# ScalarE reads s2 in VectorE's PSUM bank instead of in a copy of its own

## The chip, the cores and the metric

The kernel runs on one core of a Trainium2 chip. Its engines are TensorE (PE, matrix products), VectorE (DVE), ScalarE (ACT), GpSimd (POOL) and SyncE (SP, which issues DMAs). PE writes its products into PSUM, which has eight banks of 512 float32 values per partition; DVE and ACT read and write PSUM and SBUF, and in this kernel POOL works on SBUF alone. The metric is the device time of one execution in microseconds (us).

## The reference

Four graph layers follow each other on an input x of 64 graphs, 256 nodes and 128 features, each with a layer norm, a ReLU and a residual. The first layer holds nearly all the work:

```python
W1, W2 = (W[:, :F], W[:, F:])
s1 = jnp.einsum('bkf,ef->bke', x, W1)
s2 = jnp.einsum('bkf,ef->bke', x, W2)
pre = s1[:, :, None, :] + s2[:, None, :, :] + b_lin
h = jnp.where(pre >= 0, pre, ALPHA * pre)
e = jnp.einsum('bije,e->bij', h, a) + bias
attn = jax.nn.softmax(e, axis=2)
out = jax.nn.sigmoid(jnp.einsum('bij,bjf->bif', attn, x))
```

For every pair of nodes (i, j) of a graph, and for each of 256 features e, s1 of node i and s2 of node j are added and put through a leaky ReLU; a weighted sum over e gives one number per pair. That is 64 x 256 x 256 x 256 elements. The other layers (a second attention layer, an attention with tanh and exp, and a gated recurrent layer of five steps) are small beside it.

## The kernel before

**Pairs.** The features lie on the partitions, in two halves (`ec` 0 and 1). For one node i and one half, the value for all 256 nodes j is one instruction over a 128x256 tile: s2 against a per-partition scalar of node i. Three engines make such tiles, into buffers named r (twelve of them; each holds eight tiles), with forms that differ by terms which are put right elsewhere:

- ACT: `activation(Relu, bias=s1)`, one tile per instruction (L698);
- POOL: `tensor_scalar` with min and max against s1n, the negated s1 (L703), from the SBUF tile s2;
- DVE: `tensor_tensor` max of s2 and s1n, four tiles (128x1024, a half) or eight (128x2048, a whole) per instruction (L680).

PE multiplies each r by a window of the weights and accumulates over all of them in the bank e_ps (L764). In some batches DVE first merges the second half's value into a tile that some engine has made, by a `scalar_tensor_tensor` (L722), so that PE has fewer products to do.

**Where s2 lies.** For each graph, `senders` (or `first_head` for the first) has PE write s2 into a PSUM tile s2_ps of 128x2x256 float32, which fills a bank. Two such banks take turns in a pool that other tiles share. ACT copies it to the SBUF tile s2 (L577, L497). Inside `Pairs`, `own` says which copy an engine reads: DVE reads s2_ps. ACT, at its second piece of work on a graph, copies s2 once more, into a tile s2_act in a PSUM bank of its own (L642); its first two pieces read the SBUF tile, and all later ones s2_act. POOL reads the SBUF tile.

**The order of the work.** The program is written in an order that a planner sets while the kernel is built. A `Model` keeps one clock per engine and adds a cost in nanoseconds for each instruction: 365 for an ACT tile from PSUM, 42 more from SBUF, 454 for a POOL tile, 1131 and 2198 for DVE's half and whole, 392 for a merge. The main loop always issues the piece that can start first by these clocks; a free engine takes the next half batch of the graph. The other layers run as chains of small steps (`Chain`), which are put among the pairs at a set pace. The instructions of each engine run on the chip in the order issued. The semaphores between engines are set by the layer below the kernel, from which instruction writes and reads which tile or bank in that order; the kernel's text has none.

Of the kernel before, what the change touches and what calls it, by code (L numbers as in the profile page):

```python
# [8 lines left out]
F32 = mybir.dt.float32  # L9
# [3 lines left out]
P = 128  # L13
N = 256
# [41 lines left out]
def kernel(ctx: ExitStack, tc: tile.TileContext, ins: dict, out: bass.AP):  # L56
# [14 lines left out]
    ps_c = ctx.enter_context(tc.tile_pool(name="ps_c", bufs=1, space=bass.MemoryType.PSUM))  # L71
# [13 lines left out]
    model = Model()  # L85
# [7 lines left out]
    def act(n, pointers=0, sbuf=0, table=0, more=0):  # L93
        model.op("act", 50 + n * 0.832 + 69 * sbuf + (0, 75, 154)[pointers] + 11 * table + more)
        return nc.scalar
# [37 lines left out]
    def constant(shape, name):  # L133
        return const.tile(shape, F32, name=name)
# [20 lines left out]
    table = constant([P, 1], "table")  # L155
# [424 lines left out]
    class Pairs:  # L580
# [5 lines left out]
        def __init__(self, g, b, of, snd):  # L586
            self.g, self.b, self.of, self.snd = g, b, of, snd
            self.row = 0
            self.todo = []
            self.merges = []  # L590
            self.batches = []
            self.opened = False
            self.owned, self.by_act = {}, 0

            self.s1n_v = of["s1n"][:, :, bass.ts(b, N)].rearrange(
                "p c (k g t) -> p c g k t", k=2, g=4
            )
            self.s1n_b = of["s1n"][:, :, bass.ts(b, N)].rearrange(
                "p c (k g t) -> p c k g t", k=2, g=4
            )  # L600
# [31 lines left out]

        def own(self, who):

            if who == "dve":
                return self.snd["s2_ps"]
            if who == "act":

                self.by_act += 1
                if self.by_act == 2:  # L640
                    t = self.owned[who] = ps_c.tile([P, 2, N], F32, tag="s2_act", name="s2_act")
                    act(2 * N, table=1).copy(t, self.snd["s2"])  # L642
                if self.by_act <= 2:
                    return self.snd["s2"]
            return self.owned[who]

        def whole(self, batch, who):
            batch["halves"] += 1
# [10 lines left out]
        def make(self, who):  # L659

            if not self.todo:
                self.begin()
            batch, ec, g2 = self.todo.pop(0)
            if g2 == 0:
                batch["r"] = rp.tile([P, 4, 2, N], F32, tag="r", name="r")
                self.batches.append(batch)
            r, t = batch["r"], batch["t"]
            s2 = self.snd["s2"] if who == "pool" else self.own(who)
            s1, s1n = self.of["s1"], self.of["s1n"]
            if who == "dve":  # L670
                whole = g2 == 0 and self.todo and self.todo[0][0] is batch
                if whole:
                    self.todo.pop(0)
                n = 4 if whole else 2
                if batch["two"]:
                    s1n = self.s1n_b[:, ec, 1, 2 * g2 : 2 * g2 + n, t : t + 2].unsqueeze(3)
                else:
                    s1n = self.s1n_v[:, ec, 2 * g2 : 2 * g2 + n, :, t : t + 1]
                model.op("dve", model.WHOLE if whole else model.HALF)
                nc.vector.tensor_tensor(  # L680
                    r[:, 2 * g2 : 2 * g2 + n, :, :],
                    s2[:, ec : ec + 1, :].unsqueeze(1).to_broadcast([P, n, 2, N]),
                    s1n.to_broadcast([P, n, 2, N]),
                    ALU.max,
                )
                if whole:
                    if batch["merged"]:
                        self.merges.append((model.t[who] + LAG[who], batch, 0))
                        g2 = 1
                    else:  # L690
                        self.whole(batch, who)
            else:
                for g, ic, i in self.nodes(batch, g2):
                    if g > 2 * g2 or ic:
                        yield
                    if who == "act":
                        model.op("act", model.TILE["act"] + 42 * (s2 is self.snd["s2"]))
                        nc.scalar.activation(  # L698
                            r[:, g, ic, :], s2[:, ec, :], AF.Relu, bias=s1[:, ec, i : i + 1]
                        )  # L700
                    else:
                        model.op("pool", model.TILE["pool"])
                        nc.gpsimd.tensor_scalar(  # L703
                            r[:, g, ic, :], s2[:, ec, :], FLT_MAX, s1n[:, ec, i : i + 1],
                            ALU.min, ALU.max,
                        )
            if batch["merged"]:
                self.merges.append((model.t[who] + LAG[who], batch, g2))
            else:
                self.whole(batch, who)  # L710
# [601 lines left out]
```

## Time and profile before

| | |
|---|---|
| median of 3 runs | 5020.07 us (5019.8 to 5020.6) |
| profiled execution | 5019.59 us, span 5017.8 us |
| granted TensorE clock, mean | 0.999 |
| instructions | 176,085 |
| DMA | 29.56 MB, mean 6 GB/s |
| copies into s2_act (L642) | 64, 70.2 us busy, 1097 ns mean of a row |
| ACT reads of the SBUF tile s2 (L698) | 512, 298.2 us busy, 1006 ns mean of a row |

How to read it: a group of instructions has its line, engine, operation, tiles (output <- inputs), shapes and count; then busy time, the mean length of one row in ns, and the idle time just before them with what ended it. Rows of one engine overlap: an instruction is on record from its start to its last write, and the next starts before that, so the step from one to the next is shorter than the mean row. A line of the timeline merges equal instructions that follow each other: start, length from the first start to the last end, and their number; an idle time before it is in brackets, with what ended it.

### The profile page before, as it was taken

Reading aid. Unit: us, or ns where it says so; the run is one execution under the profiler, and the core shown is the slowest. Engines: PE = TensorE matmul, PEld = TensorE weight load, DVE = VectorE, ACT = ScalarE, POOL = GpSimd, SP = SyncE. Lnnn points to the kernel's source line nnn. Section 1 sums busy time; section 2 is a strip of 40 time slices with the busy share of each in tenths; the row PEclk is TensorE's granted clock in tenths of the full one; section 3 lists DMA queues with packets and bytes.
Section 4 is the critical chain, followed back from the end, with each engine's and each line's share of the span. In section 5 each row is a group of like instructions: output and inputs, shape, how many; then the busy total and the mean of one; then the engine's idle time right before and its main releaser. Section 6 shows DMA issues by size and latency. Waiting matters only on the chain.

```text
span 5017.8 us, 176085 instructions
## 1 busy us (share of the span) xinstructions
PE 4985.7 (99%) x69627; PEld 2291.3 (46%) x69627; DVE 4895.7 (98%) x8591; ACT 4922.9 (98%) x12912; POOL 4778.0 (95%) x10637
## 2 busy tenths in 40 slices
PE   9999999999999999999999999999999999999998
PEld 4444444444444444444444444444444444444444
DVE  9999999999999999999999999999999999999994
ACT  8999999999999999999999999999999999999994
POOL 8999999999999999999999999999999999999881
PEclk9999999999999999999999999999999999999999
DMA  0000000000000000000000000000000000000000
GB/s 22 4 6 2 5 6 7 6 2 6 7 6 7 2 6 6 7 6 2 6 8 4 7 4 6 6 7 4 4 6 6 7 7 2 5 5 4 4 4 8
DMA packets 56109, 29.56 MB, mean 6 GB/s; under 512 B 20336, under 2 KB 55280, under 8 KB 55280
## 3 DMA queue, kind: packets, MB, share of 16 engines
q1 hardware_dynamic: 54736, 18.04, 1.5%
q8 instruction: 546, 8.95, 0.7%
q14 instruction: 283, 2.32, 0.2%
q10 hardware_dynamic: 544, 0.26, 0.0%
HBM read 9.84 MB, written 8.45 MB: 4 GB/s over the span
## 4 chain that ended last, share of the span: by engine, by line
PE 92%; DVE 4%; ACT 3%; issue 1%; POOL 0%; DMA 0%; DVEq 0%; ACTq 0%; POOLq 0%
PE e_ps L764 56%; PE gate_ps L109 8%; PE hv_ps L109 6%; PE m_ps L109 5%; PE s_ps L109 3%; DVE r L680 3%; PE o_ps L109 2%; PE e_ps L109 2%; ACT r L698 2%; PE rc_ps L109 2%; PE hn_ps L116 1%; PE rsum_ps L109 1%; PE e_ps L116 1%; PE h_t_ps L116 1%; DVE r L722 1%
## 5 line engine op out<-in xcount | busy, mean ns | idle before, releaser
L703 POOL TENSOR_SCALAR r<-s,s1n 128x256 f32<-128x256 f32 x10012 | 4528.5, 476 | 79.4 <-PE e_ps L764 36.4
L698 ACT ACTIVATE r<-s_act,s 128x256 f32<-128x256 f32 x9664 | 4170.7, 871 | 7.6 <-PE e_ps L764 6.0
L764 PE MATMUL e_ps<-r,a_win 128*32 128x256 f32 (+1 forms) x40144 | 3258.1, 467 | 3.4 <-DVE r L680 3.3
L680 DVE TENSOR_TENSOR r<-s_ps,s1n 128x1024 f32<-128x1024 f32 (+1 forms) x1281 | 2291.0, 1824 | 3.9 <-PE e_ps L764 3.9
L764 PEld LDWEIGHTS e_ps<-r,a_win 128*32 128x32 f32 x40144 | 1279.9, 110 | 1574.3 <-issue 853.6
L722 DVE SCALAR_TENSOR_TENSOR r<-s_ps,s1n,r 128x256 f32<-128x256 f32 x4504 | 1852.6, 471 | 1.7 <-POOL r L703 1.0
L698 ACT ACTIVATE r<-s,s 128x256 f32<-128x256 f32 x512 | 298.2, 1006 | 0.1
L109 PE MATMUL m_ps<-adj_t,hn 128*32 128x256 f32 x4096 | 248.0, 381 | 1.6 <-ACT hn L1089 1.6
L455 ACT ACTIVATE h<-x,bsh,brs 128x128 f32<-128x128 f32 x384 | 229.6, 850 | 5.6 <-POOL bsh L449 4.7
L109 PEld LDWEIGHTS m_ps<-adj_t,hn 128*32 128x32 f32 x4096 | 133.0, 110 | 118.2 <-issue 32.2
L1066 ACT ACTIVATE gate_ps<-gate_ps,bz 128x512 f32<-128x512 f32 (+1 forms) x170 | 170.8, 1005 | 2.7 <-PE gate_ps L109 2.7
L1068 ACT ACTIVATE hv_ps<-hv_ps,bh 128x512 f32<-128x512 f32 (+1 forms) x170 | 166.4, 979 | 6.5 <-PE hv_ps L109 6.5
L1038 ACT COPY m_t<-m_ps 128x512 f32<-128x512 f32 (+1 forms) x170 | 161.4, 949 | 9.3 <-PE m_ps L109 9.3
L1048 ACT ACTIVATE m_ps<-gate_ps,br 128x512 f32<-128x512 f32 (+1 forms) x170 | 161.0, 949 | 8.9 <-PE gate_ps L109 7.2
L109 PE MATMUL hv_ps<-rh,u_th 128*32 128x512 f32 (+1 forms) x1360 | 168.4, 567 | 0.9 <-DVE rh L1051 0.9
L109 PE MATMUL gate_ps<-m_t,t_w_w 128*32 128x512 f32 (+1 forms) x1360 | 168.1, 568 | 0.3 <-ACT m_t L1038 0.2
L109 PE MATMUL hv_ps<-m_t,t_w_w 128*32 128x512 f32 (+1 forms) x1360 | 168.5, 567 | 0.0
L109 PE MATMUL gate_ps<-m_t,w_t 128*32 128x512 f32 (+1 forms) x1360 | 168.4, 568 | 0.0
L1089 ACT COPY hn<-hn_ps 128x512 f32<-128x512 f32 (+1 forms) x136 | 126.5, 930 | 18.2 <-PE hn_ps L116 18.0
L109 PE MATMUL gate_ps<-hf,u_t 128*32 128x512 f32 (+1 forms) x1088 | 135.4, 567 | 0.0
L109 PE MATMUL s_ps<-h0t,w_p 128*32 128x256 f32 (+1 forms) x1568 | 134.9, 445 | 0.5 <-ACT h0t L471 0.5
L447 POOL TENSOR_TENSOR brs<-bve,neg_half 128x4 f32<-128x4 f32 (+1 forms) x136 | 133.5, 982 | 0.0
(213 smaller groups left out, 4388.1 us busy)
## 6 DMA issues: line engine op xcount, KB each, us to landing
xt<-in_x_dram SPq DMA_DIRECT2D x30, 256.0 KB
out_dram<-y SPq DMA_DIRECT2D x30, 256.0 KB
row<-rows SPq DMA_DIRECT2D x128, 0.5 KB
xt<-in_x_dram SPq DMA_DIRECT2D x4, 128.0 KB
out_dram<-y SPq DMA_DIRECT2D x4, 128.0 KB
bound<-row SPq DMA_DIRECT2D x30, 2.0 KB
raw_L_gnn_w_w<-in_L_gnn_w_w_dram SPq DMA_DIRECT2D x3, 128.0 KB
adj_n<-in_adj_dram ACTq DMA_DIRECT2D x1, 256.0 KB
```

What stands on the lines that cost most here:

```text
L109: nc.tensor.matmul(out[bass.ts(c, 32), :], lhsT=lhsT[:, bass.ts(c, 32)], rhs=rhs, **flags)
L116: nc.tensor.transpose(out, src, ident)
L455: act(P, 2, 1).activation(h[:, g, :], xt[:, g, :], AF.Relu, bias=shift[:, g : g + 1], scale=rstd[:, g : g + 1],)
L680: nc.vector.tensor_tensor(r[:, 2 * g2 : 2 * g2 + n, :, :], s2[:, ec : ec + 1, :].unsqueeze(1).to_broadcast([P, n, 2, N]), s1n.to_broadcast ...
L698: nc.scalar.activation(r[:, g, ic, :], s2[:, ec, :], AF.Relu, bias=s1[:, ec, i : i + 1])
L703: nc.gpsimd.tensor_scalar(r[:, g, ic, :], s2[:, ec, :], FLT_MAX, s1n[:, ec, i : i + 1], ALU.min, ALU.max,)
L722: nc.vector.scalar_tensor_tensor(r[:, g, ic, :], self.own("dve")[:, 1, :], self.of["s1n"][:, 1, i : i + 1], r[:, g, ic, :], ALU.max, ALU.add,)
L764: nc.tensor.matmul(to, lhsT=a_win[:, sign, 31 - t : 63 - t], rhs=of, start=False, stop=self.over, skip_group_check=True,)
L1038: act(W).copy(m_t, m_ps)
L1048: act(W, 1).activation(t_r, g_ps, AF.Tanh, bias=br, scale=0.5)
L1066: act(W, 1).activation(t_z, g_ps, AF.Tanh, bias=bz, scale=0.5)
L1068: act(W, 1).activation(cand, hv_ps, AF.Tanh, bias=bh)
```

## The change

`own` gives DVE and ACT the same tile, s2_ps; the copy s2_act and the count of ACT's pieces are dropped. The planner's cost of an ACT tile loses the 42 ns for SBUF. POOL goes on reading the SBUF tile.

```diff
-            self.owned, self.by_act = {}, 0
...
         def own(self, who):
 
-            if who == "dve":
-                return self.snd["s2_ps"]
-            if who == "act":
-
-                self.by_act += 1
-                if self.by_act == 2:
-                    t = self.owned[who] = ps_c.tile([P, 2, N], F32, tag="s2_act", name="s2_act")
-                    act(2 * N, table=1).copy(t, self.snd["s2"])
-                if self.by_act <= 2:
-                    return self.snd["s2"]
-            return self.owned[who]
+            return self.snd["s2_ps"]
...
-                        model.op("act", model.TILE["act"] + 42 * (s2 is self.snd["s2"]))
+                        model.op("act", model.TILE["act"])
                         nc.scalar.activation(
                             r[:, g, ic, :], s2[:, ec, :], AF.Relu, bias=s1[:, ec, i : i + 1]
                         )
```

In the changed kernel the line numbers from L642 on are 11 lower: L698 becomes L687, L680 L669, L703 L692, L722 L711, L764 L753.

## The prediction

> **What bounds the kernel now.** I read the page's busy line first, then the groups kept apart by shape, the waits of ScalarE (ACT) and VectorE (DVE), and the timeline of the same microseconds on both engines.
>
> ```profile
> PE 4985.7 (99%) x69627; PEld 2291.3 (46%) x69627; DVE 4895.7 (98%) x8591; ACT 4922.9 (98%) x12912; POOL 4778.0 (95%) x10637
> ```
>
> All four engines are full at once; the planner has dealt the work out evenly, so no single stage sets the end. By shape, the work that touches s2 is this:
>
> ```profile
> L698 ACT ACTIVATE r<-s_act,s 128x256 f32<-128x256 f32 x9664 | 4170.7, 871 | 7.6 <-PE e_ps L764 6.0 <-POOL bmm L445 1.2
> L722 DVE SCALAR_TENSOR_TENSOR r<-s_ps,s1n,r 128x256 f32<-128x256 f32 x4504 | 1852.6, 471 | 1.7 <-POOL r L703 1.0 <-ACT r L698 0.5
> L680 DVE TENSOR_TENSOR r<-s_ps,s1n 128x2048 f32<-128x2048 f32 x738 | 1664.6, 2276 | 3.7 <-PE e_ps L764 3.7
> L680 DVE TENSOR_TENSOR r<-s_ps,s1n 128x1024 f32<-128x1024 f32 x543 | 644.2, 1210 | 0.3 <-PE e_ps L764 0.3
> ```
>
> ACT reads the bank s2_act, DVE the bank s2_ps. The last column says that ACT waited before its reads for 7.6 us in the whole run and DVE for 5.7, and no wait of ACT's reads on DVE is among them. The timeline of both engines shows why the span is short: they read side by side.
>
> ```profile
> 1009.64 4.98 ACT L698 ACTIVATE r<-s_act,s 128x256 f32<-128x256 f32 x12
> 1009.36 1.26 DVE L722 SCALAR_TENSOR_TENSOR r<-s_ps,s1n,r 128x256 f32<-128x256 f32 x3
> 1010.53 2.28 DVE L680 TENSOR_TENSOR r<-s_ps,s1n 128x2048 f32<-128x2048 f32 x1
> 1012.73 3.21 DVE L722 SCALAR_TENSOR_TENSOR r<-s_ps,s1n,r 128x256 f32<-128x256 f32 x8
> ```
>
> Twelve ACT reads run beside twelve DVE reads. Four more places give prices: the step of a read in a packed row, and what a start after a wait costs.
>
> ```profile
> 23.68 11.46 ACT L698 ACTIVATE r<-s_act,s 128x256 f32<-128x256 f32 x31
> 62.68 0.47 ACT L698 ACTIVATE r<-s_act,s 128x256 f32<-128x256 f32 x1
> ...
> 1002.95 4.37 DVE L722 SCALAR_TENSOR_TENSOR r<-s_ps,s1n,r 128x256 f32<-128x256 f32 x11
> 1007.24 1.21 DVE L680 TENSOR_TENSOR r<-s_ps,s1n 128x1024 f32<-128x1024 f32 x1
> 1008.37 0.47 DVE L722 SCALAR_TENSOR_TENSOR r<-s_ps,s1n,r 128x256 f32<-128x256 f32 x1
> ```
> ```profile
> 4980.82 0.45 ACT L1048 ACTIVATE m_ps<-gate_ps,br 128x256 f32<-128x256 f32 x1 [1.27 <-issue]
> 4981.30 0.42 DVE L1051 SCALAR_TENSOR_TENSOR rh<-m_ps,hf 128x256 f32<-128x256 f32 x1 [0.29 <-ACT m_ps L1048]
> ...
> 4935.81 0.48 DVE L834 TENSOR_SCALAR elu_m<-xh_ps,c_L_gnn_bi 128x256 f32<-128x256 f32 x1 [0.46 <-PE xh_ps L109]
> 4936.39 0.45 ACT L836 ACTIVATE xh_ps<-xh_ps,c_L_gnn_bi 128x256 f32<-128x256 f32 x1 [0.99 <-DVE elu_m L834]
> ```
>
> An ACT read alone takes 0.47 us, and one in a row steps by (11.46 - 0.47)/30 = 0.366. A DVE merge (L722) takes 0.47 alone and steps by (4.37 - 0.47)/10 = 0.39. The half read steps by 1008.37 - 1007.24 = 1.13 and the whole read by 1012.73 - 1010.53 = 2.20, each with a row 0.08 longer. A handover from ACT to DVE takes 4981.30 - 4981.27 = 0.03; the one from DVE to ACT here, where the wait is an instruction of its own, 4936.39 - 4936.29 = 0.10.
>
> **What the change does, part by part.** It removes 64 copies into s2_act (0.49 us a step, 31 us of ACT). It also ends the 512 ACT reads that went to SBUF before and beside the copy: they cost 298.2 us in their rows and step by about 0.40, so about 17 us go. The planner hears of 42 ns less on these and shifts a little work: in the instruction listing of the changed kernel ACT has 10,272 reads (before 10,176), POOL 9,980 (10,012), DVE 714 whole, 553 half and 4,592 merging reads (738, 543, 4,504). Taken alone, this is a gain of below 50 us on ACT.
>
> What it adds is not in the diff but in that listing, which names the semaphores that each instruction waits for. Two shortened excerpts from the middle (L687 is the old L698, L669 the old L680):
>
> ```
> ACT  L687 Activation r<-s_ps,s 128x256 [waits DVE]
> ACT  L687 Activation r<-s_ps,s 128x256 x4
> ACT  L687 Activation r<-s_ps,s 128x256 [waits DVE]
> DVE  L669 TensorTensor r<-s_ps,s1n 128x1024 [waits Activation]
> DVE  L669 TensorTensor r<-s_ps,s1n 128x2048 [waits Activation]
> ```
>
> Wherever, in program order, the reader of an s2_ps bank changes from one engine to the other, the second waits for the other's last read: 4,786 such waits on ACT and 4,795 on DVE. By its value, each names exactly the latest read of the other engine. Program order is the planner's order of time, in which both engines read alternately, and the planner knows nothing of the waits. So the two engines take turns over the bank, 9,581 times, and their read times add up instead of lying side by side. Behind a waiting read its engine's whole queue stands: for ACT the copies and activations of the other layers, for DVE the normalisations and gates; PE then waits for the batches, and POOL for the buffers that PE frees.
>
> The sum, made on the chain of turns:
> - Reads at packed steps: ACT 10,272 x 0.366 = 3,760; DVE 714 x 2.20 + 553 x 1.13 + 4,592 x 0.39 = 1,571 + 625 + 1,791 = 3,987. Together 7,747 us.
> - First read of a turn, not overlapped with its predecessor: ACT 4,786 x (0.47 - 0.366) = 498; DVE 4,795 x 0.08 = 384. Together 882.
> - Handovers: 7,486 waits sit on the reading instruction, at 0.03: 225. 2,095 sit on a wait instruction of their own, at 0.10: 210. Together 435.
> - Other work inside a turn, between two reads of the same turn, stretches it: 630 instructions of ACT, 267 us at their packed steps, and 70 of DVE, 17 us: 284.
> - Other work between two turns lies beside the other engine's turn: 1,804 instructions of ACT (817 us) and 2,603 of DVE (856 us). Turn by turn, only 29 us of it are longer than the turn that covers them. If nothing of it were covered it would cost 1,673.
> - Ends without turns, as now: 15.6 us ahead of the first read and 5,017.8 - 4,907.5 = 110 after the last: 126.
> - At changes of graph two banks are in use and 205 reads (some 78 us) have no partner to wait for; I take back 50.
> - Waits of the two engines for PE and POOL: between 100 and 4,870 us the waits views add up to some 50 us now. Other engines get slack (PE 4,986 and POOL 4,778 us of work in a span almost twice as long), so I keep 50, between 0 and twice that.
>
> Sum: 7,747 + 882 + 435 + 284 + 29 + 126 - 50 + 50 = 9,503 us of span. The profiled execution lasted 5,019.6 against a span of 5,017.8, and the median of the runs is 5,020.1, so 2 us lie around it: 9,505. That is 1.89 times the time before.
>
> Here a rule speaks against the change. The Trainium skill, "PSUM — Partial Sum Buffer", section on bank collisions, says that two engines must not touch one bank and quadrant at once, two readers included, that the hardware raises an error rather than stalling, and that compilers put a dependency between any such pair. In this case's own terms, the timeline above shows the two readers in two banks, and the listing shows the dependency for one bank; no row shows a collision. By the rule alone the waits cannot be had away, and the sum stays as above.
>
> A second page gives other prices for a turn. The skill's "ScalarE: Activation LUTs", section on what a table load costs, has an ACTIVATE with a pointer bias at about 280 ns + 0.833 ns per element, 493 ns here, and 93 ns of overlap between neighbours. By it ACT's reads would be 10,272 x 0.400 + 4,786 x 0.093 = 4,554 instead of 4,258 and the sum some 9,800. The rows say 0.366 and 0.47, and I go by them.
>
> **Rivals.**
> Turns are cheaper than priced. A wait may be met earlier than the profile's end of a row, so that restart and handover vanish: 9,505 - 882 - 435 = 8,190 at the least. For it: the 0.03 handover shows how little the semaphore itself takes. Against it: single rows of 0.47 after a wait are what the trace shows. With 0.453 (the shortest ACT read) and 0.03 for every handover, 82 + 147 go: 9,275. Below 9,250: 0.07.
>
> More comes into the open than I count. If a quarter of the 1,673 us between turns is not covered, because it waits itself for PE or the other engine, the time is 9,920; with half, 10,340. In the same case I put PE's clock: the page's clock row has it at full speed nearly everywhere, but in the drained end the granted clock falls to 0.62 in the 3.5 us after a stretch with PE busy for 0.74 of 3.4 us. PE would now be idle almost half the time. At half clock throughout its 4,986 us become 9,970 plus ends, some 10,100, which would make PE the bound. Against it: 12 buffers of r keep PE fed, and its share of some 53% is spread over the turns. Above 9,950: 0.09.
>
> Not slower. The waits would have to be met whenever an engine reaches them. Then only 48 us of ACT's work go; shared over four full engines that is 12, so 5,008, or 4,972 if all of it reaches the end. It decides if ACT's and DVE's reads need not overlap to fit the span; they need 3,760 and 3,987 us, 154% of 5,018, so at least 2,700 us of overlap have to go somewhere. A program whose waits are not obeyed on the chip would be the only way: 0.02.
>
> **How the numbers follow.** The forecast of taking turns at the prices above has 0.82; its bounds are 9,250 (restart and handover at their lowest) and 9,950 (a quarter of the covered work exposed), and those are also the range, leaving 0.18 out. A change of 0.2%, 10 us, is about what these runs can tell from none; the cheapest case of turns is hundreds of times that, so faster and same share the last rival: 0.01 each, slower 0.98.
>
> **What would show it.** In the changed kernel's waits, ACT r L687 waiting for DVE r L669 and L711 (the merges) leads with some 4,000 us, and DVE waiting for ACT r L687 with as much. ACT and DVE fall to about 55% busy, PE to 53%, POOL to 50%. The chain of work that ended last, PE at 92% now, goes to ACT r L687 with some 45% and DVE r with some 45%. Packed ACT reads stay at 0.366 inside a turn and 0.47 alone. The prediction is wrong if ACT and DVE rows on s2_ps overlap in the timeline, if PE stays above 90% busy at a lower clock, or if much of ACT's idle time ends with PE or POOL.

## The result, and the profile after

The changed kernel takes 9514.56 us (median of 4 runs, 9513.97 to 9516.47), the kernel before 5019.93 beside it: a ratio of 1.8958, 95% interval 1.8936 to 1.8981. The forecast was 9505 us, in a range of 9250 to 9950. The profiled execution took 9516.47 us, with a span of 9514.6 and a mean granted TensorE clock of 0.864 (0.999 before).

The busy line of the page after the change:

```profile
PE 6600.1 (69%) x69451; PEld 2550.4 (27%) x69451; DVE 5325.8 (56%) x8665; ACT 5403.3 (57%) x12944; POOL 4776.4 (50%) x10605
```

No engine is full any more. ACT and DVE each stand a little above half of the span, which is what two engines that take turns look like. The groups by shape of the changed kernel, with the idle time before each in the last column:

```profile
L687 ACT ACTIVATE r<-s_ps,s 128x256 f32<-128x256 f32 x10272 | 4330.0, 479 | 4030.4 <-DVE r L669 2031.7 <-DVE r L711 1926.2 <-PE e_ps L753 23.9
L711 DVE SCALAR_TENSOR_TENSOR r<-s_ps,s1n,r 128x256 f32<-128x256 f32 x4592 | 2141.0, 482 | 2534.9 <-ACT r L687 2425.4 <-POOL r L692 100.7 <-POOL bsh L449 2.6
L669 DVE TENSOR_TENSOR r<-s_ps,s1n 128x2048 f32<-128x2048 f32 x714 | 1635.1, 2291 | 900.3 <-ACT r L687 836.0 <-POOL r L692 25.4 <-PE e_ps L753 23.5
L669 DVE TENSOR_TENSOR r<-s_ps,s1n 128x1024 f32<-128x1024 f32 x553 | 675.6, 1224 | 626.2 <-ACT r L687 603.3 <-POOL r L692 12.2 <-PE e_ps L753 6.3
```

Before, ACT's reads had 7.6 us of idle time ahead of them; now they have 4030, of which 3958 end with a DVE read. DVE's reads wait 3865 us for ACT's. These are readers that wait for readers: neither uses what the other has made there. A merge does need a tile r that ACT may have made, but that is not what it waits for: in the listing 3,653 of DVE's turns open with a merge, and in none of them had the ACT read that is waited for written the tile that is merged. PE and POOL appear with little. The rows themselves have hardly become longer (2291 ns for the whole read, 2276 before). ACT's mean row is shorter, 479 ns instead of 871, because rows no longer pile up: before, 8,941 of the 10,176 reads started more than 0.2 us before their predecessor's end, now 42 of 10,272 do.

The turns can be read off the timeline of ACT and then of DVE, changed kernel, around 2000 us:

```profile
2004.60 1.57 ACT L687 ACTIVATE r<-s_ps,s 128x256 f32<-128x256 f32 x4 [0.81 <-DVE r L669]
2006.04 0.68 ACT L1037 ACTIVATE m_ps<-gate_ps,br 128x512 f32<-128x512 f32 x1
2008.52 2.30 ACT L687 ACTIVATE r<-s_ps,s 128x256 f32<-128x256 f32 x6 [1.81 <-DVE r L669]
```
```profile
2006.20 2.29 DVE L669 TENSOR_TENSOR r<-s_ps,s1n 128x2048 f32<-128x2048 f32 x1 [0.77 <-ACT r L687]
2008.40 0.68 DVE L1040 SCALAR_TENSOR_TENSOR rh<-m_ps,hf 128x512 f32<-128x512 f32 x1
2010.85 1.23 DVE L669 TENSOR_TENSOR r<-s_ps,s1n 128x1024 f32<-128x1024 f32 x1 [1.76 <-ACT r L687]
```

ACT's four reads end at 2006.17 and DVE starts at 2006.20. DVE's read ends at 2008.49 and ACT starts at 2008.52. The gate (L1037 on ACT) and the product L1040 on DVE run during the other engine's turn, so they cost nothing. This pattern fills the span from 16 to 9409 us.

### The profile page after: what moved, and what is told of

Read it like the earlier page. It is cut to its first block, busy times and chain, and to the rows that moved or that the text cites. A ratio compares the mean times of both kernels' runs of the same rounds, so it can differ in the third digit from the quotient of the medians.

```text
span 9514.6 us, 177932 instructions
## 1 busy us (share of the span) xinstructions
PE 6600.1 (69%) x69451; PEld 2550.4 (27%) x69451; DVE 5325.8 (56%) x8665; ACT 5403.3 (57%) x12944; POOL 4776.4 (50%) x10605
## 5 line engine op out<-in xcount | busy, mean ns | idle before, releaser
L687 ACT ACTIVATE r<-s_ps,s 128x256 f32<-128x256 f32 x10272 | 4330.0, 479 | 4030.4 <-DVE r L669 2031.7
L692 POOL TENSOR_SCALAR r<-s,s1n 128x256 f32<-128x256 f32 x9980 | 4527.2, 474 | 2976.6 <-PE e_ps L753 2359.2
L753 PE MATMUL e_ps<-r,a_win 128*32 128x256 f32 (+1 forms) x39968 | 4260.6, 518 | 429.4 <-ACT r L687 243.1
L711 DVE SCALAR_TENSOR_TENSOR r<-s_ps,s1n,r 128x256 f32<-128x256 f32 x4592 | 2141.0, 482 | 2534.9 <-ACT r L687 2425.4
L669 DVE TENSOR_TENSOR r<-s_ps,s1n 128x2048 f32<-128x2048 f32 (+1 forms) x1267 | 2309.9, 1825 | 1526.5 <-ACT r L687 1439.3
L753 PEld LDWEIGHTS e_ps<-r,a_win 128*32 128x32 f32 x39968 | 1463.9, 121 | 2890.6 <-issue 1334.5
L109 PE MATMUL gate_ps<-m_t,t_w_w 128*32 128x512 f32 (+1 forms) x1360 | 271.4, 886 | 628.4 <-ACT m_t L1027 628.3
L109 PE MATMUL hv_ps<-m_t,t_w_w 128*32 128x512 f32 (+1 forms) x1360 | 192.8, 617 | 117.1 <-DVE rh L1040 116.6
L109 PE MATMUL s_ps<-g_t,h_t 128*32 128x256 f32 x1024 | 88.4, 472 | 139.8 <-ACT hv L947 88.4
L116 PE MATMUL hn_ps<-ident,hf 128*128 128x128 f32 x512 | 96.2, 314 | 126.5 <-DVE hf L1067 125.5
L116 PE MATMUL h_t_ps<-ident,h 128*128 128x128 f32 x256 | 73.5, 360 | 127.2 <-ACT h L455 125.2
L109 PE MATMUL rc_ps<-e_t,y 128*32 128x256 f32 x1024 | 82.0, 473 | 99.4 <-DVE self_t L905 99.4
```

Of the source, the lines that this page charges most:

```text
L109: nc.tensor.matmul(out[bass.ts(c, 32), :], lhsT=lhsT[:, bass.ts(c, 32)], rhs=rhs, **flags)
L116: nc.tensor.transpose(out, src, ident)
L669: nc.vector.tensor_tensor(r[:, 2 * g2 : 2 * g2 + n, :, :], s2[:, ec : ec + 1, :].unsqueeze(1).to_broadcast([P, n, 2, N]), s1n.to_broadcast ...
L687: nc.scalar.activation(r[:, g, ic, :], s2[:, ec, :], AF.Relu, bias=s1[:, ec, i : i + 1])
L692: nc.gpsimd.tensor_scalar(r[:, g, ic, :], s2[:, ec, :], FLT_MAX, s1n[:, ec, i : i + 1], ALU.min, ALU.max,)
L711: nc.vector.scalar_tensor_tensor(r[:, g, ic, :], self.own("dve")[:, 1, :], self.of["s1n"][:, 1, i : i + 1], r[:, g, ic, :], ALU.max, ALU.add,)
```

## The experiments

The theory is that ACT and DVE take turns over the one bank, because the build puts a dependency between their reads of it: the listing has one at each change of reader. The rivals: the planner's order in the changed kernel is a bad one; reads of a shared bank are slow in themselves; TensorE's lower clock lengthens the span; the program is slow as a whole, not by the number of turns. Where no interval is given below, a kernel was executed once; repeated executions of one kernel here lie within 8 us of each other.

**The shared bank alone undone, in the same order of work.** Relative to the changed kernel:

```diff
         def own(self, who):
+            if who == "act":
+                if not hasattr(self, "mine"):
+                    self.mine = ps_c.tile([P, 2, N], F32, tag="s2_act", name="s2_act")
+                    nc.scalar.copy(self.mine, self.snd["s2"])
+                return self.mine
             return self.snd["s2_ps"]
```

> The changed kernel in its own order of work (the same reads, merges and products; the planner is not told of the copy), but ACT copies s2 into a bank of its own ahead of its first piece on a graph and reads that. The one thing undone is the shared bank. Theory (turns): the four full engines again, 5,020, with up to 64 x (0.49 + 0.2) = 44 us for copies that the planner did not count: 5,020 to 5,064, say 5,045 us. Rival (the planner's changed order costs): near 9,510 us.

Measured: 5047.4 us, 1.0056 times the kernel before (1.004 to 1.0073). In this run's groups the same 10,272 ACT reads and 4,592 merges have next to no idle time:

```profile
L692 ACT ACTIVATE r<-s_act,s 128x256 f32<-128x256 f32 x10272 | 4487.8, 1029 | 8.1 <-PE e_ps L758 3.6 <-ACT s_act L637 0.4
...
L716 DVE SCALAR_TENSOR_TENSOR r<-s_ps,s1n,r 128x256 f32<-128x256 f32 x4592 | 1889.8, 472 | 3.4 <-ACT r L692 1.5 <-POOL r L697 0.7
```

The order of the changed kernel is as good as the one before; the shared bank alone costs 4467 us. The 28 us over the kernel before are about the size of 64 copies (31 us at 0.49) that the planner was not told of.

**No copy, and no shared bank: ACT reads SBUF.** Relative to the changed kernel:

```diff
         def own(self, who):
-            return self.snd["s2_ps"]
+            return self.snd["s2_ps" if who == "dve" else "s2"]
...
-                        model.op("act", model.TILE["act"])
+                        model.op("act", model.TILE["act"] + 42)
```

> ACT makes no copy of s2, as in the changed kernel, but reads the SBUF tile s2, so no bank is shared and the listing has no waits of a reader on a reader. Theory (the engines take turns over the bank): no turns, so the time is set by the four full engines again. ACT reads step by 0.40 instead of 0.366 us, the planner gives ACT 9,452 tiles instead of 10,176 and merges 544 fewer, so PE has 544 more products at some 0.11 us: 5,020 + 58, about 5,080 us (5,030 to 5,150). Rival 1 (the missing copy, or the planner's changed order, is what costs): about 9,500 us. Rival 2 (TensorE's lower clock costs): the clock should stay at 1.0 here, so this run does not tell it from the theory.

Measured: 5085.4 us (before, beside it, 5023.4). ACT's reads wait for next to nothing:

```profile
L687 ACT ACTIVATE r<-s,s 128x256 f32<-128x256 f32 x9452 | 3963.8, 512 | 7.1 <-PE e_ps L753 6.9
```

Dropping the copy starts no turns as long as ACT reads something that DVE doesn't. The 62 us go with what the planner moves from the slower ACT to the other engines: PE, 99% busy, has 5,047 us of work instead of 4,986.

**Sharing in every other group of graphs.** Relative to the kernel before:

```diff
-            if who == "dve":
+            if who == "dve" or self.g % 2 == 0:
                 return self.snd["s2_ps"]
```

> The kernel before, but in every other group of graphs (5,152 of 10,232 ACT reads) ACT reads the bank s2_ps; in the others it has its copy. The listing has 4,827 turns, half of the changed kernel's 9,581. Theory (turns): the cost is local to the graphs that share, so about half of 4,495 us: 5,020 + 4,495 x 4,827/9,581 = 7,285 us (7,150 to 7,400). Rival (the program falls into a slow state as a whole, through the planner or the clock): near 9,500, or a time that does not go with the number of turns.

Measured: 7280.2 us, against 7285 from the theory. Its groups hold both kinds of ACT read in one program, 5,152 with the wait and 4,824 without:

```profile
L698 ACT ACTIVATE r<-s_ps,s 128x256 f32<-128x256 f32 x5152 | 2180.1, 489 | 2021.8 <-DVE r L680 1035.2 <-DVE r L722 950.2 <-PE e_ps L764 12.1
L698 ACT ACTIVATE r<-s_act,s 128x256 f32<-128x256 f32 x4824 | 2063.0, 862 | 5.2 <-PE e_ps L764 5.1
```

The cost is local to the graphs that share.

**Sharing for ACT's first two pieces on a graph.** Relative to the kernel before:

```diff
                 if self.by_act <= 2:
-                    return self.snd["s2"]
+                    return self.snd["s2_ps"]
```

> Only ACT's first two pieces on each graph (512 of 10,204 reads) read the bank s2_ps; then it makes its copy from SBUF and reads that, as in the kernel before. The listing has 226 turns instead of 9,581. Theory (turns): (9,515 - 5,020)/9,581 = 0.47 us per turn, 226 of them: some 106, so about 5,130 us (5,050 to 5,250; the buffers between the engines may hide a part). Rival (a program that shares a bank is slow as a whole, by its order or its clock, not by the number of turns): near 9,500, or no difference from 5,020.

Measured: 5166.7 us, 143 over the kernel before in place of 106. The waits view has both sides:

```profile
ACT r L698 <- DVE r L680: 134.7, 82, 2.5
DVE r L680 <- ACT r L698: 125.1, 113, 2.6
```

The waits here are on average longer than in the changed kernel (134.7/82 = 1.6 us for ACT, against 3958/4535 = 0.9): the DVE reads that ACT waits for are all L680, whose rows are 1.2 to 2.3 us, and none is a 0.47 us merge. A fixed price per turn is therefore too coarse; what counts is the reading time that no longer overlaps. Five per cent of ACT's reads were enough to cost 2.9%.

**Longer turns, the same reads.** Relative to the changed kernel, ACT's four tiles and DVE's two merges no longer give way in between:

```diff
-                    if g > 2 * g2 or ic:
+                    if who != "act" and (g > 2 * g2 or ic):
                         yield
...
-                if g > 2 * g2:
+                if g < 0:
                     yield
```

> The changed kernel, but ACT's four tiles of a half batch are issued one after the other, and DVE's merges two by two, so the listing has 4,326 turns instead of 9,581, over the same bank and with as many reads (10,284 on ACT). Theory (turns): read times still add up, 7,743 us, but 5,255 turns less at 0.10 for the restart and 0.037 for the handover are 720 us less: about 8,790 us (8,650 to 8,950). Rival 1 (reads of a shared bank are slow in themselves): unchanged, about 9,510. Rival 2 (TensorE's clock): unchanged or longer, as PE's idle gaps grow.

Measured: 8626.8 us, in place of 8790 and 23 us below the range given. Less than half the turns take off 888 us, and 3600 us over the kernel before remain. Most of that is the theory's main term: 10,284 ACT reads and 5,878 DVE reads at packed steps are 7743 us however they are bunched, some 2,700 more than the kernel before takes. The 160 us that I missed lie mostly in what stretches a turn. From the first to the last read, ACT's turns here take 4059 us; less its reads at packed steps (10,284 x 0.3655 = 3759) and 2,265 restarts at 0.109, 53 are left for other work inside them. The same sum for the changed kernel leaves 278. Pieces issued together have less other work between them. That is 225 us less; the gaps between turns are 43 shorter than expected too, while DVE's turns and the two ends take some 50 us more each.

**Half of PE's pair products left out.** Relative to the changed kernel:

```diff
-                for g in range(4):
+                for g in range(2):
                     to, of = self.e_ps[bass.ts(g, 32), ic, :], r[:, g, k, :]
```

> The changed kernel with half of PE's products of the pairs left out (two of the four groups of rows), so its scores are incomplete; all reads, turns and waits of ACT and DVE stay. Theory (turns): the same time, 9,500 within 40 us. Rival 2 (TensorE's clock, at 0.864 on average, lengthens the span): PE's 6,600 us of busy time fall by about a third, and the time falls by 200 us or more; if PE were a bound at its lower clock, down to 8,200.

Measured: 9527.4 us, at a mean clock of 0.843. Half of the pair products less, and the time does not fall. So neither PE's lower clock nor its work sets this span. One surprise is in the page's busy line:

```profile
PE 6416.8 (67%) x49467; PEld 2445.9 (26%) x49467; DVE 5325.0 (56%) x8665; ACT 5413.0 (57%) x12944; POOL 4799.1 (50%) x10605
```

With 19,984 matmul rows less than the changed kernel, PE's busy time falls by 183 us only. On this starved PE, busy time says little about how much work it has.

**The other way to unshare: DVE reads SBUF.** Relative to the changed kernel, in its own order of work:

```diff
         def own(self, who):
-            return self.snd["s2_ps"]
+            return self.snd["s2_ps" if who == "act" else "s2"]
```

> The changed kernel, instruction for instruction in the planner's order (same counts of tiles, merges and products), but DVE reads the SBUF tile s2, so that ACT alone reads the bank s2_ps and no reader waits for a reader. Theory (turns): the time falls back near that of the kernel before; PE has 88 products less (9 us) and ACT 48 us less to do, so about 5,010 us if DVE reads SBUF at the price of PSUM (2.20, 1.13, 0.39 us), and some 5% more of DVE's 3,987 us, 200 us, if it reads SBUF slower: 4,990 to 5,250. Rival (it is the planner's order in the changed kernel, not the shared bank): about 9,510 us, since the order is the same.

Measured: 7744.2 us, 1.543 times the kernel before (1.5404 to 1.5456). Both expectations missed. The reader-on-reader waits are gone: ACT's reads have 116.6 us of idle time before them, 1.4 of it ended by DVE. Something else is the bound:

```profile
L692 POOL TENSOR_SCALAR r<-s,s1n 128x256 f32<-128x256 f32 x9980 | 7207.6, 740 | 26.3 <-DVE v_rep L299 9.2 <-PE e_ps L753 3.5
...
L711 DVE SCALAR_TENSOR_TENSOR r<-s,s1n,r 128x256 f32<-128x256 f32 x4592 | 2784.9, 656 | 699.2 <-POOL r L692 656.4 <-ACT r L687 41.0
```

POOL's tile went from 476 to 740 ns, and POOL is busy for 98% of the span. I took this for an effect of DVE on POOL and tested it without ACT's part.

**DVE reads SBUF, with ACT in its own bank.** Relative to the kernel before:

```diff
             if who == "dve":
-                return self.snd["s2_ps"]
+                return self.snd["s2"]
```

> The kernel before, with ACT in its own bank, but DVE reads the SBUF tile s2, as in the run of 7,744 us, in which ACT read s2_ps. Theory for that run (POOL's tiles take 0.72 instead of 0.45 us each when DVE takes both of its tensors from SBUF beside it, and POOL becomes the bound; ACT's bank has no part in it): again about 7,740 us (7,600 to 7,900), POOL's rows at some 740 ns, POOL 98% busy. Rival (ACT's reads of the bank that PE wrote made that run slow): about 5,020 us.

Measured: 7791.5 us, with the same picture on POOL and DVE:

```profile
PE 6105.3 (78%) x69627; PEld 2565.5 (33%) x69627; DVE 5920.8 (76%) x8591; ACT 4987.8 (64%) x12912; POOL 7605.5 (98%) x10637
...
L703 POOL TENSOR_SCALAR r<-s,s1n 128x256 f32<-128x256 f32 x10012 | 7191.6, 736 | 39.4 <-PE e_ps L764 15.7 <-DVE v_rep L299 9.9 <-issue 0.2
...
L722 DVE SCALAR_TENSOR_TENSOR r<-s,s1n,r 128x256 f32<-128x256 f32 x4504 | 2733.7, 656 | 784.6 <-POOL r L703 709.4 <-ACT r L698 74.1
...
L680 DVE TENSOR_TENSOR r<-s,s1n 128x2048 f32<-128x2048 f32 x738 | 1734.5, 2369 | 61.0 <-PE e_ps L764 56.6 <-POOL r L703 4.4
```

ACT's bank has no part in it. In the kernel before POOL's rows lie between 467 and 493 ns from the 5th to the 99th percentile; here half of them are over 600 and 834 over 1500. Each of the 834 runs beside an L680 read of DVE, and 97% of their time on average lies beside DVE's reads of SBUF. This agrees with the Trainium skill, "SBUF — State Buffer", in its section on the two sides of SBUF: DVE and GpSimd share one port pair, a DVE instruction with two SBUF inputs holds it against a GpSimd instruction that reads SBUF for its whole length, and the loser blocks. The runs show the blocking and its price; that a lock is the mechanism is the page's statement.

**PE makes ACT's copy.** Relative to the kernel before, two products per graph take the place of ACT's copy:

```diff
-                    act(2 * N, table=1).copy(t, self.snd["s2"])
+                    h_t = flat(self.of["h_t"][:, 2 * self.b : 2 * self.b + 2, :])
+                    for ec in range(2):
+                        mm(
+                            t[:, ec, :], lhsT=w_p[:, 1, bass.ts(ec, P)], rhs=h_t,
+                            start=True, stop=True,
+                        )
```

> The kernel before, but PE makes the tile s2_act by a second product (8 matmuls per graph, 512 in all) instead of ACT copying it from SBUF. No bank is shared by readers. Theory (turns): nothing like 9,500, since the change's aim, ACT without the copy, is had without turns. ACT gains 31 us, PE has 160 products more in the listing at some 0.11 us: PE is the fullest engine, so 5,020 + 17, about 5,037 us (5,005 to 5,060). Rival (ACT's copy is what kept the engines apart): far above.

Measured: 5041.3 us, 1.0048 times the kernel before (1.0036 to 1.0061). The change's aim, an ACT that copies nothing, is to be had without turns; it gains nothing. PE, as full as ACT, now has 5,004 us of work instead of 4,986, which is most of the 23 us lost.

**The copy ahead of ACT's first piece.** Relative to the kernel before:

```diff
-                if self.by_act == 2:
+                if self.by_act == 1:
...
-                if self.by_act <= 2:
+                if self.by_act <= 1:
```

> The kernel before, but ACT copies s2 into its own bank before its first piece on a graph, so 256 instead of 512 reads go to SBUF. Gain of ACT: 256 x 0.034 = 9 us, shared over four engines 2 us; the listing has 40 products less on PE, 4 us. Theory: 5,015 us (5,005 to 5,025), at the edge of what can be told. Rival (the first reads after the copy wait for it, 0.2 us x 64 = 13 us): 5,030.

Measured: 5024.4 us, 1.0011 times the kernel before (1.0002 to 1.002). The gain of 5 us did not come; 6 us were lost, between the two expectations. The idle time before ACT's reads is 6.8 us, no more than before, so a wait for the copy is not what the profile shows. The cause of these 6 us is open.

## Why the prediction was right, point by point

The mechanism stood in every run that could have felled it: where the bank was shared the time went with the reads that no longer overlap, and where it wasn't, hardly any such wait was left. Two times missed their ranges, the one with longer turns by 23 us and the one with DVE on SBUF by far, for a cause that has nothing to do with the bank. The sum itself can be laid beside the trace. For this I put all 16,131 reads of s2_ps of the changed kernel in order of start: from the first to the last, each instant belongs to a turn or to the gap between two turns. In us:

| term, as predicted | predicted | measured |
|---|---|---|
| ACT's turns: reads 3,760, restarts 498, other work inside 267 | 4,525 | 4,566 |
| DVE's turns: reads 3,987, restarts 384, other work inside 17 | 4,388 | 4,467 |
| gaps: handovers 435, uncovered work 29, other waits 50, less 50 at changes of graph | 464 | 360 |
| ends: before the first read and after the last | 126 | 122 |
| span | 9,503 | 9,515 |

- **The waits.** They were read from the changed kernel's listing, not from the diff. The profile has them where they were expected: 3958 us on ACT and 3865 on DVE, some 4,000 each.
- **Restarts.** A turn of n ACT reads lasts 0.473 + (n - 1) x 0.365 us, as priced. The reading behind the 0.366 was not quite right: in the row of 31 the reads start every 0.356 us while their rows grow from 0.525 to 0.780, and it is their ends that step by 0.365. DVE's restart was put at 0.08 from the tail of a packed row; a read that has waited is longer than its step by 0.09 (0.484 against 0.392, 2.292 against 2.198). That is most of the 79 us missing in DVE's line.
- **Handovers.** The two prices were right: the median gap is 0.034 us from ACT to DVE and 0.035 from DVE to ACT, with a second group at 0.10 and 0.095 where the wait is an instruction of its own. Short gaps add up to 461 us (435 predicted) and longer ones to 24 (29). The sum is smaller than mine because reads overlap by 125 us where two banks are in use, and I took back 50, and because the 50 us of other waits that I added are not found between turns. The turns are 120 us over my sum and the gaps 104 under it, so the 0.1% is partly luck; by themselves ACT's and DVE's lines are within 2%, the ends within 4% and the gaps 22% off.
- **What hides.** That 1,673 us of other work lie behind the other engine's turns held: the 24 us of longer gaps are all that shows of it. Inside the turns ACT has 278 us more than its reads and restarts, 267 predicted.
- **PE.** The clock fell as the rival feared, with 2,585 us at half, and PE's busy share is 69% where I said 53%. The rival's price was wrong: leaving out half of the pair products left the time as it was.
- **The chain.** I expected some 45% each for ACT's and DVE's reads. The page's chain after the change names about a quarter of the span (ACT r L687 9%, L711 and L669 5% each) and loses the rest, so the share can't be tested there; the waits and the timeline carry it.
- **The rule that speaks against the change.** The Trainium skill, "PSUM — Partial Sum Buffer", section on bank collisions, says that two engines must be kept apart on a bank and quadrant, readers too. No run shows what the chip does without the waits: they come from the build, and taking the wait alone away was not tried.

## What to carry to other kernels

Here the build ordered two engines that read one PSUM bank against each other, so their read times added: before giving a PSUM tile a second reader on another engine, add up both engines' reads of it and compare the sum with the span. (The tile s2_ps fills its bank, so no run tells whether the build goes by the tile or by the bank. The SBUF tile s2 had two readers, ACT and POOL, in the run without a copy, and 6.9 of ACT's 7.1 us of waits there end with PE.) Here a copy of 31 us kept 3,760 and 3,987 us of reads side by side. Look at the waits in the built program as well as at the diff: an edit that only names another tile can add thousands of them.

## What was unexpected of the hardware

When DVE takes both of its tensors from SBUF beside a POOL that reads SBUF, POOL's 128x256 tile goes from 476 to 736 ns on average and DVE's merge from 471 to 656: some 2,700 us on a kernel of 5,020, in two kernels with different banks for ACT. And PE's busy time hardly moved, from 6,600 to 6,417 us, when 29% of its matmuls were left out.
